# Glances ahead of the second tanh, looks in two pairs, and earlier x loads in a gated graph network kernel

## The chip, the core and the metric

The kernel runs on one core of a Trainium2 chip. The metric is device time in microseconds (us). Before the change three runs took 1787.79, 1788.79 and 1789.32 us, so the median is 1788.79.

## What is computed

For 16 graphs of 1024 nodes and 128 channels, two layers are applied, each behind a layer norm and a relu, and each added to its input. The first is a gated graph network of four steps; the second is four graph convolutions, each with a batch norm over all graphs. Cut to what matters:

```python
# layer 0: gated, per graph
h = relu(layernorm(x))
for i in range(4):
    m = adj.T @ (h @ weight[i])
    r = sigmoid(m @ w_ir + h @ w_hr + b_r)
    z = sigmoid(m @ w_iz + h @ w_hz + b_z)
    n = tanh(m @ w_in + b_in + r * (h @ w_hn + b_hn))
    h = (1 - z) * n + z * h
x = x + h * mask
# layer 1: convolutions
h = relu(layernorm(x))
for i in range(4):
    h = relu(adj @ (h @ W[i]) + b[i])
    h = gamma[i] * (h - mean(h)) / sqrt(var(h) + eps) + beta[i]
x = x + h
```

The adjacency holds only zeros and ones in this data. The kernel has a fast path that needs values whose low 16 bits are zero, and a general path that is taken at the end if any value had other low bits. So every adjacency row is inspected once, beside the work.

## The kernel before

**Two streams.** In the gated layer two graphs are in flight: stream `sa` takes the even graphs, `sb` the odd ones. A half-step (`half_step(one, two)`, called in turn with the roles swapped) does the gates of one step of stream `two` on ScalarE (ACT) and VectorE (DVE), and the aggregation of one step of stream `one` on TensorE (PE). On PE a half-step is 12 gate products of 128x512 (`products`, L993, two matmuls each) for the two halves of the nodes, hf = 0 and 1, and then 32 aggregation matmuls (`aggregate_rows`, L524). A graph takes four steps, so eight half-steps make one period, in which both streams finish a graph and start the next. The streams are one half-step apart.

**The gates of one half.** `reset_gate` is the r sigmoid on ACT (L1011), then two DVE operations, r * (g_hn + b) (L1012) and the sum with g_xn (L1013). `candidate` is the tanh on ACT (L1016), `update_gate` the z sigmoid on ACT (L1020). `less` (L1029), and the product and sum in `mixed` (L1033, L1034), are on DVE. Then `half_away` transposes the new half on DVE (L720) and sends it to HBM, from where it is read back in another layout for the next step (`cross_h`, `n_h`, `pair_out`, `pair_in`, `h_in`). The four PSUM banks g_r, g_z, g_hn and g_xn are used by both halves in turn: PE may write g_hn of the second half only when L1012 of the first has read it, and g_z only when the z sigmoid has. `high` and `low` (L926 or L942, tile ghw) split the aggregation's input of the other stream in two parts, on ACT and DVE. At the end of a half-step ACT copies the aggregation out of PSUM (tile m, L955); the next half-step's products need m.

**Rows of the next graph.** In the half-step with a stream's last gates (`self.i == 3`), `fetch` loads the first four of the next graph's eight adjacency rows (512 KB each, SyncE queue, SP, L572) into four staging buffers. `first_four` rounds them on GpSimd (POOL, L577). `last_four`, called after the second z sigmoid, inspects the four on ACT (`glance`: an activation with an accumulated sum, L586), loads rows 4 to 7 into the same four buffers, each behind the glance and the rounding that free it, and rounds them. Rows 4 to 7 of `sa` are inspected in the next half-step on DVE (`look`: a maximum over the row, L610), those of `sb` in the next half-step on ACT. Both streams share the four buffers, so `fetch` of `sb` waits for the looks at the rows of `sa`.

**The order.** In this part the order on each engine is the order of the program. Work that belongs beside another half-step is put on an agenda: `at(n, place, go)` files it, `due(place)` runs it when half-step n comes to that place. Places in order are ins, start, beside0 (after `reset_gate(0)`), mid (after `half_away(0)`, behind a small POOL copy, pace), beside1 (after `reset_gate(1)`), outs, gap and end (after `half_away(1)`). The looks at `sa` rows are at start, ahead of all gates on DVE; the glances at `sb` rows 4 to 7 are at gap, ahead of the copy of m on ACT.

**The input x of a coming graph.** `plan` files its load (`next_load`, POOL queue, L539) at mid of half-step n + 5, its statistics on DVE (L664) at start of n + 6. The tile it uses is freed by the graph that ends: its `blocks` (ACT, L680) read it last, at beside0 and beside1 of n + 4. POOL also casts rows to bf16 (tile half, L615) for the transposes of the adjacency that SP issues, and stores them (adjT_d), xmid and ymid.

Of the kernel before, what the change touches and what calls it, by code (L numbers as in the profile page):

```python
# [341 lines left out]
def exact_path(  # L342
# [24 lines left out]
    NB = N // P  # L367
# [165 lines left out]
    with ExitStack() as st:  # L533
# [36 lines left out]
        def stage_rows(b, stage, js):  # L570
            for j in js:
                nc.sync.dma_start(stage[j % 4], adj[b][j * P : (j + 1) * P, :])  # L572
# [7 lines left out]
        def glance(b, stage, js):  # L580

            junk = work.tile([P, N], BF16, tag="junk", name=f"junk{b}_{js[0]}", bufs=1)
            for j in js:
                lows = stage[j % 4].bitcast(U16).rearrange("p (n t) -> p n t", t=2)[:, :, 0]
                k = b * NB + j
                nc.scalar.activation(junk, lows, AF.Copy, accum_out=low[:, k : k + 1])  # L586
# [19 lines left out]
        def look(b, row, j, part=0):  # L606

            lows = row.bitcast(U16).rearrange("p (n t) -> p n t", t=2)[:, :, 0]
            k = (b + part * B) * NB + j
            nc.vector.tensor_reduce(low[:, k : k + 1], lows, axis=AX.X, op=ALU.max)  # L610
# [67 lines left out]
        def norm_blocks(xt, y, nt, ks):  # L678
            for k in ks:
                nc.scalar.activation(  # L680
                    y[:, k * P : (k + 1) * P], xt[:, k, :], AF.Relu, bias=nt[3][:, k, :], scale=nt[2][:, k, :]
                )
# [43 lines left out]
        def tail_sums(b, xt, hT, parts=None):  # L726

            for hf in range(NH):
                if parts:
                    pt = by_nodes(parts[hf])  # L730
                else:
                    pt = tmp(f"pt_x{b}_{hf}")
                    for q in range(BH):
                        k = hf * BH + q
                        nc.tensor.transpose(pt[:, q * P : (q + 1) * P], hT[:, k * P : (k + 1) * P], ident)
                    pt = four_ways(pt)
                for q in range(BH):
                    k = hf * BH + q
                    xk = xt[:, k, :].rearrange("p (a c) -> p a c", a=4)
                    mask = maskT[:, b * NB + k : b * NB + k + 1]  # L740
                    nc.vector.scalar_tensor_tensor(xk, pt[:, q, :, :], mask, xk, ALU.mult, ALU.add)
            return norm_stats(xt, f"mid{b}")
# [5 lines left out]
        def y_mid(b):  # L748
            return work.tile([P, N], F32, tag="h", name=f"y_mid{b}", bufs=7)
# [20 lines left out]
        class Stream:  # L770
# [54 lines left out]
            def plan(self, n, tail=None):  # L825

                if tail:
                    b, xt, hT, parts = tail
                    end = {}

                    def sums():
                        end["norm"] = tail_sums(b, xt, hT, parts)

                    def blocks(hf):
                        if hf == 0:
                            end["y"] = y_mid(b)
                        norm_blocks(xt, end["y"], end["norm"], range(hf * BH, (hf + 1) * BH))

                    at(n + 2, "gap", sums)
                    at(n + 3, "mid", lambda: store_xmid(b, xt))  # L840
                    at(n + 3, "gap", lambda: norm_factors(end["norm"]))
                    at(n + 4, "beside0", lambda: blocks(0))
                    at(n + 4, "beside1", lambda: blocks(1))
                    at(n + 5, "mid", lambda: store_ymid(b, end["y"]))
                if self.b + 2 < B:
                    at(n + 5, "mid", self.next_load)
                    at(n + 6, "start", self.next_sums)
                    at(n + 6, "gap", self.next_factors)
                    at(n + 7, "beside0", lambda: self.next_blocks(0))
                    at(n + 7, "beside1", lambda: self.next_blocks(1))  # L850
                    at(n + 7, "end", self.ins_away)

            def fetch(self):

                if self.i == 3 and self.b + 2 < B and not written[0]:
                    if self is sa:
                        t = turned_tile(f"stage{self.b + 2}").bitcast(F32)
                        room[0] = [t[:, 2 * q : 2 * q + 2, :].rearrange("p a n -> p (a n)") for q in range(4)]
                    self.stage = room[0]
                    stage_rows(self.b + 2, self.stage, range(4))  # L860

            def first_four(self):
                if self.stage:
# [2 lines left out]
            def last_four(self):  # L866
                if self.stage:
                    b, stage, self.stage = self.b + 2, self.stage, None
                    glance(b, stage, range(4))
                    stage_rows(b, stage, range(4, NB))  # L870
                    self.rows += round_rows(b, stage, range(4, NB))

                    def looks():
                        for j in range(4, NB):
                            look(b, stage[j % 4], j)

                    if self is sa:
                        at(clock[0] + 1, "start", looks)
                    else:
                        at(clock[0] + 1, "gap", lambda: glance(b, stage, range(4, NB)))  # L880

            def take(self):
                self.xt, self.y = self.next_x, self.next_y
# [173 lines left out]
        clock = [3]  # L1057

        def at(n, place, go):
            agenda.setdefault((n, place), []).append(go)  # L1060

        def due(place):
            for go in agenda.pop((clock[0], place), ()):
                go()

        def first_step(one, two, gated, halfway):

            feed.next_step()
            if one is sa:
                feed.jobs = transposes([(s.b, s.rows) for s in (sa, sb)])  # L1070
            one.split_step()
            feed.some(2)
            two.gate_step(0)
            two.half_away(0)
            if feed.full or (clock[0], "mid") in agenda:
                mids(two)
            feed.some(1)
            two.gate_step(1)
            two.half_away(1)
            gated()  # L1080
            one.agg_step(0)
            halfway()
            feed.some(NB if one is sa else 1)
            one.agg_step(1)
            two.finish()
            clock[0] += 1
# [8 lines left out]
        def half_step(one, two, gated=None, halfway=None):  # L1095

            feed.next_step()
            counts = (2, 1, 1)
            if one is sb and one.i == 0:
                feed.jobs = transposes([(s.b, s.rows) for s in (sa, sb)])  # L1100
                counts = (0, 0, 0)
            elif two is sb and two.i == 0:
                counts = (2, 2, 1)
            elif two is sa and two.i == 1 and two.across:
                counts = (3, 1, 1)
            due("ins")
            due("start")
            if one.i > 0:
                one.halves_back()
            else:  # L1110
                one.hw = hw_tiles(one.b, f"ghw{one.b}_0")
            two.fetch()
            feed.some(counts[0])
            two.products(0)
            two.reset_gate(0)
            due("beside0")
            two.candidate(0)
            two.less(0)
            one.high(0)
            two.update_gate(0)  # L1120
            one.low(0)
            two.mixed(0)
            two.half_away(0)
            two.first_four()
            if feed.full or (clock[0], "mid") in agenda:
                mids(two)
            one.high(1)
            feed.some(counts[1])
            two.products(1)
            two.reset_gate(1)  # L1130
            due("beside1")
            one.low(1)
            two.candidate(1)
            two.less(1)
            two.update_gate(1)
            two.last_four()
            two.mixed(1)
            two.half_away(1)
            due("outs")
            due("gap")  # L1140
            due("end")
            if gated:
                gated()
            one.agg_step(0)
            if halfway:
                halfway()
            feed.some(counts[2])
            one.agg_step(1)
            two.finish()
            clock[0] += 1  # L1150

        sa, sb = Stream(0), Stream(1)
        every = {getattr(mybir.EngineType, e) for e in ("PE", "DVE", "Activation", "Pool", "SP")}
        prep = st.enter_context(tc.tile_pool(name="prep", bufs=1))
        with tc.manual_schedule(engines=every):
# [20 lines left out]
            stage = keep.tile([P, NB, N], BF16, tag="adjT", name="stage", bufs=1).bitcast(F32)  # L1176
            quarters = [[stage[:, 2 * j : 2 * j + 2, :].rearrange("p a n -> p (a n)")] for j in range(4)]
            late = [[work.tile([P, N], F32, tag="h", name=f"first{j}", bufs=7)] for j in range(4, NB)]
# [404 lines left out]
```

## Time and profile before

| | |
|---|---|
| median of three runs | 1788.79 us |
| the profiled execution, its own time | 1789.26 us |
| its span, first to last instruction | 1787.5 us |
| mean granted TensorE clock | 0.999 |
| a glance on ACT (84 of them) | 1.057 us and 0.187 us to read the sum |
| a look on DVE at a staged row | 1.220 us |
| staged row load, issue to landing | 3.5 / 5.7 / 7.9 us (least, median, most) |
| waits of the statistics for x | 15.8 us, 14 times |

Times are from the page, from the answers on single tiles, and from the timeline, whose first two columns are the start and the duration in us, followed by engine, line, operation, written and read tiles, shape and count; in brackets stands the idle time of the engine before it and what ended it. Lines of POOLq, SPq and ACTq are queue entries, DMA issues among them. Positions in the run are in us from the span's start. The gated part runs from the start to about 1175 us, the convolutions from there.

### The profile page before, as it was taken

The page shows a single profiled execution, that of the slowest core. Times are in us where ns is not written, and L with a number is a line of the kernel's source. Part 1 is how long each engine was busy: PE and PEld are TensorE (multiplying, and loading weights), DVE is VectorE, ACT ScalarE, POOL GpSimd, SP SyncE. Part 2 cuts the span into 40 slices and gives each one's busy share as a digit, 9 for nine tenths or more (in the row PEclk, how much of TensorE's full clock was granted, in tenths as well). Part 3 has the DMA queues.
Part 4 walks back from the last instruction along what each step waited for, and adds up shares of the span by engine and source line. Part 5 has one row for each costly group of instructions (what it writes and reads, how often), then busy time and mean ns, then how long its engine had stood idle before and what let it go on. Part 6 is the DMA issues. An engine that isn't in the chain of part 4 may idle for free. (4 is left out here: it accounts for less than half of the span.)

```text
span 1787.5 us, 22335 instructions
## 1 busy us (share of the span) xinstructions
PE 1759.3 (98%) x6734; PEld 1191.7 (67%) x6734; DVE 1305.9 (73%) x2310; ACT 1107.6 (62%) x1713; POOL 379.3 (21%) x417
## 2 busy tenths in 40 slices
PE   9999999999999999999999999999999999999997
PEld 6565655565656565556555556577778888888886
DVE  7677877887887787887797787676666666666665
ACT  5356556556566556665655655476777767768765
POOL 4314323332331331422432333010100000000011
PEclk9999999999999999999999999999999999999999
DMA  7467657777676676776756768788766575767667
GB/s 259 135 175 262 189 163 272 179 208 241 204 200 213 223 212 197 245 202 202 260 169 186 265 174 227 256 287 311 271 228 241 207 253 201 245 224 245 238 217 268
DMA packets 363617, 400.16 MB, mean 224 GB/s; under 512 B 158188, under 2 KB 239888, under 8 KB 363488
## 3 DMA queue, kind: packets, MB, share of 16 engines
q1 hardware_dynamic: 342736, 323.59, 57.6%
q0 software_dynamic: 20224, 74.80, 11.3%
q8 instruction: 55, 0.90, 0.2%
q14 instruction: 74, 0.61, 0.1%
q10 hardware_dynamic: 528, 0.26, 0.0%
HBM read 267.47 MB, written 97.52 MB: 204 GB/s over the span
## 5 line engine op out<-in xcount | busy, mean ns | idle before, releaser
L524 PE MATMUL pm<-row,ghw 128*128 128x512 f32 x2048 | 503.6, 402 | 0.7 <-DVE ghw L926 0.6
L524 PEld LDWEIGHTS pm<-row,ghw 128*128 128x128 f32 x2048 | 383.8, 188 | 106.6 <-issue 29.2
L1016 ACT ACTIVATE r<-r,vecs 128x512 f32<-128x512 f32 x128 | 92.6, 723 | 255.0 <-DVE r L1013 253.1
L524 PE MATMUL pc_m<-wide,chw 128*128 128x512 f32 x1024 | 245.3, 395 | 0.0
L615 POOL CAST half<-row 128x1024 bf16<-128x1024 f32 x128 | 147.4, 1161 | 361.1 <-DMA adjT<-half 347.9
L524 PEld LDWEIGHTS pc_m<-wide,chw 128*128 128x128 f32 x1024 | 190.4, 188 | 41.9 <-issue 3.8
L524 PE MATMUL pc_g_r<-wide,chw 128*128 128x512 f32 x464 | 186.9, 403 | 0.3 <-ACT chw L501 0.3
L524 PE MATMUL pc_g_z<-wide,chw 128*128 128x512 f32 x464 | 181.0, 390 | 0.0
L577 POOL CAST row<-stage 128x1024 fp32r<-128x1024 f32 x112 | 128.6, 1156 | 243.7 <-DMA stage<-in_adj_dram 232.2
L1012 DVE SCALAR_TENSOR_TENSOR r<-g_hn,vecs,r 128x512 f32<-128x512 f32 x128 | 93.3, 729 | 117.9 <-ACT r L1011 66.9
L955 ACT COPY m<-pm 128x512 f32<-128x512 f32 x128 | 68.4, 585 | 163.5 <-PE pm L524 163.5
L1313 DVE CAST wide<-block 128x1024 fp32r<-128x1024 bf16 x160 | 109.9, 692 | 75.5 <-PE pc_m L524 48.3
L1313 DVE CAST wide<-packed 128x1024 fp32r<-128x1024 bf16 x160 | 110.1, 691 | 71.9 <-PE pc_g_z L524 53.5
L1311 ACT CAST wide<-packed 128x1024 fp32r<-128x1024 bf16 x96 | 100.6, 1048 | 58.5 <-PE pc_m L524 29.7
L993 PE MATMUL g_r<-m,w_mT 128*128 128x512 f32 x256 | 132.0, 597 | 3.4 <-ACT m L955 2.9
L1311 ACT CAST wide<-block 128x1024 fp32r<-128x1024 bf16 x96 | 100.7, 1049 | 53.9 <-PE pc_g_z L524 27.7
L993 PE MATMUL g_z<-m,w_mT 128*128 128x512 f32 x256 | 130.7, 592 | 0.0
L993 PE MATMUL g_xn<-m,w_mT 128*128 128x512 f32 x256 | 130.7, 592 | 0.0
L1361 DVE BATCH_NORM_STATS2 stats<-feat 128x6 f32<-128x512 f32 x128 | 84.1, 686 | 47.0 <-ACT feat L1360 45.9
L1029 DVE TENSOR_TENSOR h<-h,r 128x512 f32<-128x512 f32 x96 | 83.8, 872 | 41.9 <-ACT r L1016 41.8
L1033 DVE TENSOR_TENSOR h<-h,z 128x512 f32<-128x512 f32 x128 | 107.8, 842 | 6.8 <-ACT z L1020 0.2
L1011 ACT ACTIVATE r<-g_r,brz 128x512 f32<-128x512 f32 x128 | 87.9, 686 | 39.1 <-PE g_r L993 38.8
(186 smaller groups left out, 2830.5 us busy)
## 6 DMA issues: line engine op xcount, KB each, us to landing
block<-adjT_d SPq DMA_DIRECT2D x256, 256.0 KB, 4.7
packed<-adjT_d SPq DMA_DIRECT2D x256, 256.0 KB, 5.5
stage<-in_adj_dram SPq DMA_DIRECT2D x120, 512.0 KB, 5.7
adjT_d<-adjT POOLq DMA_DIRECT2D x16, 2048.0 KB, 7.7
cross_h<-t_h SPq DMA_DIRECT2D x92, 256.0 KB, 2.2
n_h<-cross_h SPq DMA_DIRECT2D x368, 64.0 KB, 2.0
xmid_d<-x POOLq DMA_DIRECT2D x16, 512.0 KB, 6.9
y<-ymid_d POOLq DMA_DIRECT2D x16, 512.0 KB, 5.4
```

Of the source, the lines that this page charges most:

```text
L524: nc.tensor.matmul(pm[hf], hw[s][:, j * P : (j + 1) * P], rows[j][:, hf * HALF : (hf + 1) * HALF], start=(j == 0 and s == 0), stop=(j == N ...
L577: nc.gpsimd.tensor_copy(t, stage[j % 4])
L615: nc.gpsimd.tensor_copy(t, row.bitcast(F32))
L993: nc.tensor.matmul(po, wT[:, i, g * C : (g + 1) * C], rhs, start=start, stop=stop)
L1011: nc.scalar.activation(r, pr, AF.Sigmoid, bias=brz[:, 3 * i : 3 * i + 1])
L1012: nc.vector.scalar_tensor_tensor(r, phn, b_hn(i), r, ALU.add, ALU.mult)
L1016: nc.scalar.activation(self.r, self.r, AF.Tanh, bias=b_in(self.i))
L1029: nc.vector.tensor_sub(ho, hin, self.r)
L1033: nc.vector.tensor_mul(ho, ho, self.z)
L1311: nc.scalar.copy(r, t)
L1313: nc.vector.tensor_copy(r, t)
L1361: nc.vector.bn_stats(stats[:, b * NH + hf, :], dst)
```

## The change

It changes when rows are inspected and loaded, and when x is loaded:

- `fetch` loads rows 0 and 1 only; rows 2 and 3 are loaded in a new `fetch_more`, after `reset_gate(0)`.
- `first_glances` inspects rows 0 and 1 on ACT after `reset_gate(1)`, in front of the second half's tanh. `last_four` inspects rows 2 and 3 where it inspected all four.
- The looks at rows 4 to 7 of `sa` become two pairs: 4 and 5 at start, 6 and 7 at a new place looks, behind `reset_gate(0)` and ahead of `fetch_more`.
- The glances at rows 4 to 7 of `sb` become two pairs: 4 and 5 at beside1, 6 and 7 at gap.
- `next_load` moves from mid of half-step n + 5 to a new place late of n + 4, right behind beside1. The two half-steps at the start in which it was the only thing at mid lose their pace copy.

In the built program PE and SP have the same instructions in the same order as before.

```diff
-                    at(n + 5, "mid", self.next_load)
+                    at(n + 4, "late", self.next_load)
...
                     self.stage = room[0]
-                    stage_rows(self.b + 2, self.stage, range(4))
+                    stage_rows(self.b + 2, self.stage, range(2))
+
+            def fetch_more(self):
+                if self.stage:
+                    stage_rows(self.b + 2, self.stage, range(2, 4))
...
                     b, stage, self.stage = self.b + 2, self.stage, None
-                    glance(b, stage, range(4))
+                    glance(b, stage, range(2, 4))
                     stage_rows(b, stage, range(4, NB))
                     self.rows += round_rows(b, stage, range(4, NB))
 
-                    def looks():
-                        for j in range(4, NB):
-                            look(b, stage[j % 4], j)
-
                     if self is sa:
-                        at(clock[0] + 1, "start", looks)
+                        for place, js in (("start", (4, 5)), ("looks", (6, 7))):
+                            at(clock[0] + 1, place, lambda js=js: [look(b, stage[j % 4], j) for j in js])
                     else:
-                        at(clock[0] + 1, "gap", lambda: glance(b, stage, range(4, NB)))
+                        for place, js in (("beside1", (4, 5)), ("gap", (6, 7))):
+                            at(clock[0] + 1, place, lambda js=js: glance(b, stage, js))
+
+            def first_glances(self):
+                if self.stage:
+                    glance(self.b + 2, self.stage, range(2))
...
             two.gate_step(1)
             two.half_away(1)
+            due("late")
             gated()
...
             due("beside0")
+            due("looks")
+            two.fetch_more()
             two.candidate(0)
...
             due("beside1")
+            two.first_glances()
+            due("late")
             one.low(1)
             two.candidate(1)
```

## The prediction, made before the changed kernel ran

> **What bounds the kernel now.** I read the page first, then who waited for whom with the PE filter, then the timeline of single half-steps, then the `low`, `stage` and `x` tiles.
>
> ```profile
> PE 1759.3 (98%) x6734; PEld 1191.7 (67%) x6734; DVE 1305.9 (73%) x2310; ACT 1107.6 (62%) x1713; POOL 379.3 (21%) x417
> PE g_z L993 <- ACT z L1020: 5.0, 8, 0.7
> PE g_hn L993 <- DVE r L1012: 4.6, 6, 1.2
> PE g_r L993 <- ACT m L955: 2.9, 4, 1.0
> ```
>
> PE is the bound, and its idle time is nearly all in three waits of the gated part (us in total, times, longest). These idle figures are too small, because the end of a matmul is modelled. I therefore count from start to start in the PE timeline. A gate matmul starts 0.429 us after the one before it (24 per half-step), an aggregation matmul 0.227 us after (32 per half-step): 24 x 0.429 + 32 x 0.227 = 17.56 us. Indeed 38 of the half-steps from 98 us on last 17.57 us, measured from the first g_r<-h to the next half-step's. That is the floor, and no edit here touches PE. What is above it repeats every eight half-steps, seven times, in three neighbours, which I call B, C and D (A is the half-step before B):
>
> - B (starts 151.0, 293.4, 437.0, 580.1, 725.1, 866.8, 1010.5): 19.07, 19.95, 19.65, 19.64, 18.33, 19.02, 19.95. Above the floor: 1.50 + 2.38 + 2.08 + 2.07 + 0.76 + 1.45 + 2.38 = 12.62 us.
> - C (170.0, 313.3, ...): 0.32 + 0.33 + 0.38 + 0.36 + 0.35 + 0.35 + 0.38 = 2.47 us.
> - D (187.9, 331.2, 474.6, 617.7, 761.3, 903.7, 1048.4): 0 + 0.32 + 0.12 + 1.08 + 0 + 1.30 + 1.03 = 3.85 us.
>
> Together 18.94 us. Two single ones stand apart: 0.89 at 636.3 and 1.51 at 1137.3.
>
> The timeline of one B, with the loads that lead to it:
>
> ```profile
> 290.04 3.87 SPq L572 DMA_DIRECT2D stage<-in_adj_dram  x4
> 293.62 1.22 DVE L610 TENSOR_REDUCE low<-stage 128x1 f32<-128x1024 uint16 x1 [1.08 <-DMA stage<-in_adj_dram]
> 295.33 1.22 DVE L610 TENSOR_REDUCE low<-stage 128x1 f32<-128x1024 uint16 x1 [0.49 <-DMA stage<-in_adj_dram]
> 298.24 2.59 DVE L610 TENSOR_REDUCE low<-stage 128x1 f32<-128x1024 uint16 x2 [1.69 <-DMA stage<-in_adj_dram]
> 300.74 0.74 DVE L1012 SCALAR_TENSOR_TENSOR r<-g_hn,vecs,r 128x512 f32<-128x512 f32 x1
> 301.54 1.13 PE L993 MATMUL g_hn<-h,w_hhT 128*128 128x512 f32 x2 [1.15 <-DVE r L1012]
> 304.18 1.12 PE L993 MATMUL g_z<-h,w_hhT 128*128 128x512 f32 x2 [0.66 <-ACT z L1020]
> ```
>
> Four looks, each waiting for its row, keep DVE until 300.74. Only then does L1012 read the g_hn bank, which PE wants back at about 300.2 for the second half; tanh and z follow late, so g_z waits too. The looks wait because the four row loads start at 290.04 only, one per glance. The start of a D:
>
> ```profile
> 899.34 0.72 ACT L1016 ACTIVATE r<-r,vecs 128x512 f32<-128x512 f32 x1 [5.44 <-DVE r L1013]
> 900.54 1.04 ACT L586 ACTIVATE junk<-stage 128x1024 bf16<-128x1024 uint16 x1
> 904.07 1.06 ACT L586 ACTIVATE junk<-stage 128x1024 bf16<-128x1024 uint16 x1
> 905.13 1.05 ACT L955 COPY m<-pm 128x512 f32<-128x512 f32 x2
> 905.74 1.13 PE L993 MATMUL g_r<-m,w_mT 128*128 128x512 f32 x2 [1.00 <-ACT m L955]
> ```
>
> ACT idles 5.44 us in front of tanh, then does four glances after z, and the copy of m, due at 903.7, comes 1.4 us late. The start of a C is the same in small (0.35).
>
> **What the Trainium skill says.** "Perfetto Trace Analysis", Tensor Engine Instruction (MATMUL, LD_WEIGHTS): the end of a matmul is an estimate, and ACT and DVE are strict FIFO. The trace agrees: PE counts as busy 18.09 of 19.90 us in a B that is 2.38 above the floor, and L1012 stands behind looks that it doesn't need. "SBUF — State Buffer", SBUF: two separate sides: DVE and GpSimd take a shared port pair exclusively, and the loser blocks. The trace agrees in kind: ghw at 648.36 took 3.05 us in place of 0.69 beside two POOL casts (648.83 to 650.85), which is the 0.89 at 636.3. "DMA: Bandwidth & Descriptors", Issuing engines are not separate DMA queues: POOL's x loads interleave with SP's row loads on the same engines; no run here shows their price apart.
>
> **The change part by part.** It adds no arithmetic: 84 glances and 28 staged looks are only moved. PE's and SP's order of instructions stays, POOL loses two pace copies of 0.19 us.
>
> *A's glances.* On ACT, y_in ends at 285.13 and tanh starts at 287.63 after an idle 2.50. A glance takes 1.18 from start to start (288.83, 290.00, 291.19), so two take 2.36 and fit; their rows have landed, since POOL casts the first from 282.36 and the second before 284.9. Tanh is not moved. Cost 0; were the rows late, tanh would shift by all lateness over 0.14, but it may end as late as 290.4, since z (0.6) and now only two glances (2.36) come before m is due at 293.4.
>
> *A's row loads.* Rows 4 and 5 now go when the first two glances end: 286.6 and 287.5 in place of 290.04 and 291.23. Rows 6 and 7 wait for the glances after z, 290.0 and 291.2 in place of 292.41 and 293.59. With the lags of before (3.6, 4.1, 5.8 and 6.0 us from issue to look) they land at 290.2, 291.6, 295.8 and 297.2. The next on SP (pair_out, pair_in, h_in) moves up 2.4 us with them.
>
> *B's looks.* DVE's transposes end at 292.5. Looks 4 and 5: to 295.0. The r sigmoid ends at 295.96, so L1012 runs to 296.7 (PE needs it at 300.2: 3.5 spare) and L1013 to 297.4. Tanh and one cast later z ends at 299.3; PE asks for g_z's bank at 301.9 (2.6 spare). Looks 6 and 7, now behind L1013: to 299.9. They make the subtraction L1029 wait 1.8, and L942, which it holds back, ends at 301.1; the aggregation needs that at 303.3. So B falls to its floor: 12.62. If row 4 and 5 were no earlier, L1012 would still be at 296.6, so this gain doesn't hang on the loads.
>
> *B's glances, the one new wait.* The two before the second tanh wait for the other stream's rows 0 and 1. Their loads stood at 299.67 behind row 7's landing and SP's h_in; now row 7 lands at 297.2 and looks 4 and 5 are done. So issue at about 297.3 and 298.0, landing with 6.3 and 5.8 us (299.67 to the cast at 306.00; 301.47 to 307.23) at 303.6 and 303.8. Glances end at 304.8 and 306.0. Queued behind them are tanh, z, two glances and the copy of m. Tanh's input is ready at 304.6 (L1012 and L1013 after t_out at 303.2), up to 306.2 if two DVE operations share with POOL casts at 1.5 us in place of 0.7. Tanh at 306.2, z until 307.5, glances until 309.9; m is due at 310.9. C's 2.47 goes, with 1.0 spare.
>
> *C's glances.* Two fill ACT's idle time before tanh (4.5 to 5.4 us), their rows landed long before. Two are left in the gap: z ends at 900.6, they at 903.0, m due 903.7. D's 3.85 goes, with 0.7 spare in the worst D.
>
> *x earlier.* POOL issues it (0.90) 15 to 17 us sooner, at about 217.2 in place of 232.92. It waits for blocks that ended at 214.93 and is behind POOL's xmid store, so it waits for nothing. Two casts behind it start 0.9 later; POOL idles 9.89 after them. The statistics lose their wait for x (15.8 us of DVE, 14 times), but those half-steps stand at 17.57, so I count 0. Without that cover the casts could push a port collision onto a ghw: 0.9 each time, or take away the one at 636.3: from -0.9 to +6.
>
> Sum: 12.62 + 2.47 + 3.85 = 18.94 less. From the profiled execution (span 1787.5, and 1.8 outside it, 1789.26) that is 1770.3; from the median 1788.79, half a microsecond lower, 1769.9. I take 1770.
>
> **The rivals.**
> - The row loads don't come earlier, because the 16 engines are the limit (DMA share 0.84 in that B). B's gain stays, D's too, but B's glances wait for rows that land at 307.2: tanh at 308.4, glances done at 312.0, m 1.1 late in each C in place of 0.35. 18.94 - 2.47 - 7 x 0.75 = 11.2 less: 1777.6. Against it: SP stood in waits for glances, not for engines.
> - No change: what B gives back is lost at the next exchange through HBM, whose cross_h and n_h transfers come no sooner. Then 1788.8, at best -3. Against: C and D wait for ACT alone.
> - Slower: B's glances hold ACT in front of tanh. They start to cost when row 1 lands after 306.1 (tanh latest 307.3), and eat all 18.94 / 7 = 2.7 per period when it lands after 308.8. Landing at 310 in every period, tanh 3.9 late, would give 7 x 3.9 = 27.3 more against 18.9 less: 1797. For it: row lags were up to 7.9 us. Against: even unadvanced it landed before 307.3.
>
> **Numbers.** Full gain (1767 to 1773.5) 0.62; partial (to 1785) 0.24; no change 0.07; slower 0.07. What a measurement can tell here is 0.2%, 3.6 us. Faster 0.86, same 0.07, slower 0.07. The low end, 1767, takes the full sum, the 0.89 and some of 1137.3; the high end, 1779, the partial case and a collision or two, leaving about 2 in 10 outside.
>
> **What would show it.** Right: B, C and D at 17.57; L1012 of a B at start + 2.7 to 3.4; row loads in two pairs some 3 us apart; no PE wait on ACT m at 313 or 903. Wrong: tanh in a B released by a glance later than start + 14; PE waiting for ACT m at the start of C; ghw of 3 us in the half-steps with x loads.

## The result and the profile after

| | before | changed |
|---|---|---|
| median, runs | 1788.82 us, 5 | 1772.93 us, 5 |
| lowest and highest | 1787.79, 1790.83 | 1772.15, 1774.21 |
| span of the profiled execution | 1787.5 us | 1772.3 us |

The ratio is 0.991, with an interval of 0.9896 to 0.9925: faster by 0.9%, or 15.9 us. The profiled execution of the changed kernel took 1774.21 us, the slowest of the five.

The page and the waits of PE of the changed kernel, in the same columns as before:

```profile
PE 1754.2 (99%) x6734; PEld 1194.8 (67%) x6734; DVE 1288.6 (73%) x2310; ACT 1108.6 (63%) x1713; POOL 373.0 (21%) x415
PE g_z L999 <- ACT z L1026: 3.6, 4, 1.8
PE g_r L999 <- ACT m L961: 0.3, 1, 0.3
```

The wait of g_hn for DVE is gone, the one of g_r for m is down to 0.3 us, but g_z still waits for z four times, with a longest wait of 1.8 us that the kernel before didn't have. Counted from start to start in the PE timeline, all seven B, all seven C and all seven D last 17.57 us. New time stands elsewhere: in three half-steps at 222.8 (19.70 us), 365.5 (17.93) and 506.4 (18.53), which are the second half-step after D. I call this place E; before the change the first E started at 223.1, and every E lasted 17.57. The fourth half-step, at 80.0, takes 19.77 in place of 18.74; like an E it follows an adjT_d store.

The timeline of the B that was shown of before, with the A in front of it, in the changed kernel (A starts at 277.6, B at 295.2):

```profile
286.87 1.04 ACT L586 ACTIVATE junk<-stage 128x1024 bf16<-128x1024 uint16 x1
288.08 4.92 SPq L572 DMA_DIRECT2D stage<-in_adj_dram  x4
293.91 2.30 DVE L610 TENSOR_REDUCE low<-stage 128x1 f32<-128x1024 uint16 x2
298.04 0.75 DVE L1018 SCALAR_TENSOR_TENSOR r<-g_hn,vecs,r 128x512 f32<-128x512 f32 x1 [1.82 <-PE g_hn L999]
299.50 2.34 DVE L610 TENSOR_REDUCE low<-stage 128x1 f32<-128x1024 uint16 x2
302.06 1.02 PE L999 MATMUL g_hn<-h,w_hhT 128*128 128x512 f32 x2
304.94 1.06 ACT L586 ACTIVATE junk<-stage 128x1024 bf16<-128x1024 uint16 x1 [1.99 <-DMA stage<-in_adj_dram]
307.22 0.71 ACT L1022 ACTIVATE r<-r,vecs 128x512 f32<-128x512 f32 x1
```

The first glance runs in front of tanh, and the first row load follows it at A + 10.5 (before: A + 14.3). The first pair of looks no longer waits for anything. L1018, which was L1012, now waits for PE and not the other way round, and the second pair of looks runs after it. The g_hn matmul follows without a gap. The glance at 304.94 waited 1.99 us for its row, and tanh still comes in time.

The start of the D shown of before:

```profile
884.09 1.05 ACT L586 ACTIVATE junk<-stage 128x1024 bf16<-128x1024 uint16 x1
888.14 0.72 ACT L1022 ACTIVATE r<-r,vecs 128x512 f32<-128x512 f32 x1 [1.74 <-DVE r L1019]
890.51 1.06 ACT L586 ACTIVATE junk<-stage 128x1024 bf16<-128x1024 uint16 x1
893.97 1.07 ACT L961 COPY m<-pm 128x512 f32<-128x512 f32 x2 [2.31 <-PE pm L524]
```

Two glances now fill most of the idle time in front of tanh (1.74 us are left of 5.44), two follow z, and ACT then waits 2.31 us for PE before it can copy m.

The worst E, from the stores in the half-step in front of it:

```profile
218.30 0.89 POOL L629 DMA_DIRECT2D adjT_d<-adjT  x1 [2.97 <-DMA adjT<-half]
219.18 0.89 POOL L752 DMA_DIRECT2D xmid_d<-x  x1
220.06 0.89 POOL L539 DMA_DIRECT2D x<-in_x_dram  x1
222.20 10.49 SPq L598 DMA_DIRECT2D n_h<-cross_h  x8
232.09 0.62 ACT L925 CAST ghw<-n_h 128x512 fp32r<-128x512 f32 x1 [3.94 <-DMA n_h<-cross_h]
232.62 0.68 ACT L1026 ACTIVATE z<-g_z,brz 128x512 f32<-128x512 f32 x1
233.35 1.12 PE L999 MATMUL g_z<-h,w_hhT 128*128 128x512 f32 x2 [1.83 <-ACT z L1026]
```

POOL issues 2 MB of adjT_d, 512 KB of xmid and now 512 KB of x in a row. Behind them SP asks for n_h, the new state in the layout that the aggregation needs. It lands late: x lands at 231.2, and the first four n_h loads at 231.4 to 231.9. The `cross_h` store that SP issued just before them, which the other four n_h loads wait for, took 9.1 us to land, against 3.1 at the same place before. The cast that waits for n_h stands in front of z on ACT, and PE waits for z. The `n_h` tile says the same of the whole run; before, then the changed kernel:

```profile
DMA to landing us min/median/max: 1.8/2.0/6.8
```

```profile
  DMA n_h<-cross_h: 29.4, 23
DMA to landing us min/median/max: 1.8/2.1/9.3
```

The median is the same, the longest landing is not, and engines now wait 29.4 us for n_h in place of 6.1.

### The profile page after: what moved, and what is told of

The parts are those of the page before. It is cut to its first block, busy times and chain, and to the rows that moved or that the text cites. A ratio compares the mean times of both kernels' runs of the same rounds, so it can differ in the third digit from the quotient of the medians.

```text
span 1772.3 us, 22314 instructions
## 1 busy us (share of the span) xinstructions
PE 1754.2 (99%) x6734; PEld 1194.8 (67%) x6734; DVE 1288.6 (73%) x2310; ACT 1108.6 (63%) x1713; POOL 373.0 (21%) x415
## 5 line engine op out<-in xcount | busy, mean ns | idle before, releaser
L615 POOL CAST half<-row 128x1024 bf16<-128x1024 f32 x128 | 141.9, 1120 | 397.8 <-DMA adjT<-half 384.6
L1018 DVE SCALAR_TENSOR_TENSOR r<-g_hn,vecs,r 128x512 f32<-128x512 f32 x128 | 93.6, 731 | 136.9 <-ACT r L1017 75.5
L1035 DVE TENSOR_TENSOR h<-h,r 128x512 f32<-128x512 f32 x96 | 83.3, 868 | 41.7 <-ACT r L1022 41.7
```

Source lines behind the costliest of these rows:

```text
L615: nc.gpsimd.tensor_copy(t, row.bitcast(F32))
L1018: nc.vector.scalar_tensor_tensor(r, phn, b_hn(i), r, ALU.add, ALU.mult)
L1035: nc.vector.tensor_sub(ho, hin, self.r)
```

## The experiments

My theory after the result: the looks and glances do all that was forecast, and what is missing comes from `sa`'s x load, whose bytes delay the n_h that follows. Rivals: the earlier row loads delay n_h; POOL's issue of the load shifts its casts and the transposes; or it was chance. The table gives, for the profiled execution of each run, the sum in us above 17.57 of all B, all C, all D and the half-steps at E's place (seven with the last period's, which has no x load), the excess of the fourth half-step over 18.74, and the median of the timed runs. The kernel before spread more widely beside these runs than beside the first (medians of 1789.9 to 1792.2), so I compare the sums first, and medians only where they were taken together.

| run | B | C | D | E | fourth | median us | ratio to before |
|---|---|---|---|---|---|---|---|
| before | 12.62 | 2.47 | 3.86 | 0.03 | 0 | 1788.82 | 1 |
| changed | 0.02 | 0.02 | 0.02 | 3.47 | 1.03 | 1772.93 | 0.991 [0.9896, 0.9925] |
| both x loads back | 0.02 | 0.02 | 0.03 | 0.83 | 0 | 1770.81 | 0.989 [0.9874, 0.9907] |
| x alone early | 13.83 | 3.58 | 2.37 | 2.42 | 1.12 | 1794.0 | 1.0018 [1.0001, 1.0035] |
| sa's x back | 0.02 | 0.02 | 0.03 | 0.03 | 0 | 1770.24 | 0.9888 [0.9871, 0.9904] |
| an eighth of x early | 0.02 | 0.02 | 0.02 | 0.68 | 0 | 1769.57 | 0.9884 [0.9868, 0.9901] |
| looks alone | 0.02 | 0.64 | 1.83 | 0.68 | 0 | 1773.56 | 0.9908 [0.9883, 0.9934] |
| glances alone | 1.10 | 0.02 | 0.02 | 0.92 | 0 | 1770.98 | 0.9886 [0.9865, 0.9907] |
| changed, again | 0.02 | 0.02 | 0.02 | 1.79 | 0.65 | 1772.61 | 0.9899 [0.9879, 0.9919] |
| sa's x twice | 0.02 | 0.02 | 0.02 | 11.16 | 1.83 | 1785.18 | 0.9965 [0.9952, 0.9978] |
| sa's x back, again | 0.02 | 0.02 | 0.02 | 1.01 | 0 | 1770.56 | 0.9885 [0.9865, 0.9905] |
| z first | 0.02 | 0.02 | 0.02 | 7.70 | 0.95 | 1778.12 | 0.9933 [0.9919, 0.9947] |
| z first, sa's x back | 0.02 | 0.02 | 0.02 | 1.05 | 0 | 1771.67 | 0.9903 [0.9889, 0.9916] |

**The x load, taken back and taken alone.** Both loads back to mid of n + 5, in the changed kernel:

```diff
-                    at(n + 4, "late", self.next_load)
+                    at(n + 5, "mid", self.next_load)
```

> The changed kernel with the x load back at mid of half-step n + 5. Theory (the new stalls before g_z, 2.13 + 0.36 + 0.96 us in the half-steps at 222.8, 365.5 and 506.4 and 0.60 at 80.0, come from sa's x load standing right behind the adjT_d and xmid stores, so that the next n_h loads land late): these stalls vanish, B, C and D stay at 17.57 us, and the time falls by 3.5 to 5 us from 1772.9, to 1768 to 1769.5. Rival (the earlier row loads and glances themselves push the n_h exchange): the stalls stay, 1772 to 1774.

Measured: no stall in any E of the first six periods, the fourth half-step is at 18.74 again, B, C and D stay. What is left at E is in the last period, where no x is loaded: there POOL issued adjT_d only 1.95 us before the half-step began, and the n_h loads landed behind it and xmid. Seven of the runs have this last stall (0.66 to 1.04 us), all with adjT_d issued 1.8 to 2.2 us ahead; in the kernel before, the changed one and the run with `sa`'s x back it went 4.7 to 5.1 us ahead, and they don't stall there. The span is 1768.7, the median 1770.81, above the expected 1768 to 1769.5. The rival falls: with the earlier rows and glances, and x back in its place, n_h stalls none of the six E that have an x load.

The reverse, only the x load and its place late, on the kernel before:

> The kernel before with the x load alone moved to late of n + 4. Theory: B, C and D keep their 18.9 us above the floor, and half-steps three after C get stalls before g_z that sum to 2 to 5 us: 1791 to 1794, slower than before by 0.1 to 0.3%. Rival (x load harmless, stalls come from the other edits): 1788 to 1789.5, no g_z stall in those half-steps.

```profile
PE g_z L993 <- ACT z L1020: 6.0, 10, 0.7
PE g_hn L993 <- DVE r L1012: 5.9, 6, 1.5
PE g_r L993 <- ACT m L955: 2.8, 5, 1.0
```

All three waits of the kernel before are there, g_z with two more. Stalls at E and in the fourth half-step sum to 3.54, but 1.27 of that is in the last period, which has no x load: there the last two n_h loads were issued just after a 256 KB load of w_hhT and landed just after it (at start + 11.3 and 11.5, w_hhT at 11.1). The 2.27 left are at the low end of what was expected. The median is 1794.0, ratio 1.0018 with an interval that just excludes 1. That the x load by itself costs is shown by the half-steps more than by the median.

**Which x load.** `sa`'s back, `sb`'s kept early:

```diff
-                    at(n + 4, "late", self.next_load)
+                    if self is sa:
+                        at(n + 5, "mid", self.next_load)
+                    else:
+                        at(n + 4, "late", self.next_load)
```

> The changed kernel with sa's x load back at mid of n + 5, sb's kept at late of n + 4. Theory (only the x load that shares a half-step with the adjT_d store hurts): no stall before g_z, 1768 to 1769.5 like the run with both back. Rival (either early x load hurts): half of the loss stays, 1770 to 1772.

E and the fourth half-step are clean. The median of 1770.24 lies in the rival's range, but the half-steps decide: no part of the stalls stays, and the run with both loads back, beside it, was no faster (1770.81). So `sb`'s early load is harmless. `sa`'s is the one that shares its half-step with the adjT_d store; that this is what tells them apart is argued from their places, and no run shows it alone.

**Bytes or queue place.** An eighth of x at late of n + 4, the rest at mid of n + 5:

```diff
-                    at(n + 4, "late", self.next_load)
+                    at(n + 4, "late", lambda: self.load_part(0, 1))
+                    at(n + 5, "mid", lambda: self.load_part(1, NB))
```

> The changed kernel with an eighth of x (64 KB) loaded at late of n + 4 and the other seven eighths at mid of n + 5: POOL issues a transfer at the same place as in the changed kernel, but with few bytes. Theory (the bytes in front of the n_h loads are the cause): the g_z stalls shrink to 0.6 us or less in all, 1768 to 1770. Rival (POOL's 0.9 us of issue shifts the casts and so the transposes and SP's order): stalls stay at 3 to 4.5 us, 1772 to 1773.5.

The stalls at E are gone but for 0.68 in the last period. POOL still issues a transfer there; with 64 KB it does no harm. The median of 1769.57 is as the theory has it. The other way, the same bytes twice:

```diff
                 self.next_x = load_x(self.b + 2, nc.gpsimd)
+                if self is sa:
+                    spare = dram.tile([N, C], F32, tag="spare", name=f"spare{self.b}")
+                    nc.gpsimd.dma_start(spare, x[self.b + 2])
```

> The changed kernel with a second transfer of the same 512 KB right behind sa's x load (DRAM to DRAM, into a spare buffer that nothing reads; it adds traffic, the output is unchanged). Theory (bytes ahead of the n_h loads): n_h lands some 2 us later in each half-step E (three after C). In the changed kernel the first ghw of the six E began at start + 9.97, 8.24, 8.84, 6.97, 7.32 and 7.06 and stalls began at about + 7.85, so all six stall, 10 to 14 us in sum, and the fourth half-step 2 us more: 1779 to 1786. Rival (the place in POOL's queue, not the bytes): 0.9 us of issue more, at most 3 us in sum: 1773 to 1776.

```profile
PE g_z L1002 <- ACT z L1029: 9.4, 8, 2.8
```

Beside it the changed kernel had 3.6 us in 4 waits. The six E last 18.39, 19.15, 19.91, 18.17, 22.25 and 17.83, 10.28 us above the floor, at the low end of the 10 to 14 expected; the excess of the fourth half-step is 1.83, up by 0.80 where 2 more were expected. The median is 1785.18. All six stall, as expected of bytes, and by more than the 3 us that a place in the queue could explain. The longest landing of an n_h load is 10.5 us.

**Chance, and the better version on the same chip.**

> The changed kernel once more, beside the two that follow on one chip. Theory: the g_z stalls again in the half-step three after C of some periods and in the fourth half-step, in sum 3 to 5 us; 2 to 4 us slower than the version with sa's x load put back. Rival (they were chance of one execution): no such stalls, the two versions equal within 1 us.

> The version with sa's x load back at mid of n + 5 and all else as changed, timed on the same chip as the changed kernel. Theory: 2 to 4 us faster than the changed kernel, E at 17.57 throughout. Rival: within 1 us of it.

Changed 1772.61, `sa`'s x back 1770.56: 2.05 us faster, at the low end of what was expected. The changed kernel again stalls in the second and third E (17.77, 18.11) and in the fourth half-step (19.39), but not in the first E, which was the largest before. At the places with an x load this is 1.39 us in sum, under the 3 to 5 expected. The rest of its 1.79 at E is the last period's stall; the version with `sa`'s x back has that too (0.99), so its E are not at 17.57 throughout, as I had expected.

The size is not mere chance: it goes with how late POOL issues adjT_d. In these two executions of the changed kernel, the store was issued 4.47, 5.33, 5.87, 5.92 and 6.06 us before the E that stalled by 2.13, 0.96, 0.54, 0.36 and 0.20 us; in the seven E that didn't stall it was issued 6.35 us or more before. Time alone doesn't do it: with `sa`'s x back, the first E lasted 17.57 with the store 4.96 us ahead. With x alone early two small stalls, of 0.22 and 0.17 us, came with the store 7.31 and 6.56 us ahead, so the order isn't strict. The store waits for the transposes of the adjacency; why they end later in some periods is not shown.

The half-step in front of the first E, in the version with `sa`'s x back:

```profile
216.62 0.89 POOL L629 DMA_DIRECT2D adjT_d<-adjT  x1 [2.68 <-DMA adjT<-half]
217.50 0.89 POOL L752 DMA_DIRECT2D xmid_d<-x  x1
221.45 6.74 SPq L598 DMA_DIRECT2D n_h<-cross_h  x8
227.37 0.62 ACT L928 CAST ghw<-n_h 128x512 fp32r<-128x512 f32 x1 [0.42 <-DMA n_h<-cross_h]
227.89 0.68 ACT L1029 ACTIVATE z<-g_z,brz 128x512 f32<-128x512 f32 x1
230.16 1.02 PE L1002 MATMUL g_z<-h,w_hhT 128*128 128x512 f32 x2
```

Without the third transfer SP issues its eight n_h loads within 6.74 us in place of 10.49, the cast waits 0.42 in place of 3.94, and z ends before PE asks for its bank. This version beats both kernels.

**The looks and the glances, each alone** on the kernel before. The looks in pairs with `fetch_more`, cut (`fetch` loads rows 0 and 1 only, as in the changed kernel):

```diff
-                        at(clock[0] + 1, "start", looks)
+                        for place, js in (("start", (4, 5)), ("looks", (6, 7))):
+                            at(clock[0] + 1, place, lambda js=js: [look(b, stage[j % 4], j) for j in js])
...
             due("beside0")
+            due("looks")
+            two.fetch_more()
```

> The kernel before with the looks in two pairs alone, and rows 2 and 3 fetched behind the second pair; all glances and the x load as before. Prediction (B's gain doesn't hang on the loads): B falls to within 0.3 us of 17.57, its 12.6 us come back; C keeps about 0.3 each and D its 3.85: 1775 to 1777.5. Rival (the looks still wait for rows that come late): B keeps a third or more of its excess, 1780 to 1785.

The glances, with `first_glances` and, not shown here, the pairs at beside1 and gap:

```diff
-                    glance(b, stage, range(4))
+                    glance(b, stage, range(2, 4))
...
+            two.first_glances()
             one.low(1)
```

> The kernel before with the glances alone split (two in front of the second tanh, those for sb in two pairs), which also brings row loads 4 and 5 forward by 3.4 us; looks all four at start, x load as before. Theory: C and D fall to 17.57; the last look ends at about start + 5.0 in place of + 7.4, L1012 is in time for PE, but tanh and z come late for g_z by 0.3 to 0.8 us in each B: 1771.5 to 1775. Rival (with four looks in front B keeps its stall): 1780 to 1784.

The wait of PE for m with the looks alone, and then its wait for z with the glances alone:

```profile
PE g_r L994 <- ACT m L956: 1.7, 5, 0.4
```

```profile
PE g_z L998 <- ACT z L1025: 1.7, 3, 0.6
```

Either takes nearly all of B away: with the looks alone 0.02 is left, with the glances alone 1.10. C and D need the glances; with the looks alone they keep 2.47 of 6.33. That is less than I expected (C some 0.3 each and D 3.85, so 1775 to 1777.5, measured 1773.56). Gates that are on time in B may leave the later glances more room, but no run shows that apart. The glances alone came out at 1770.98, just below the 1771.5 to 1775 expected: in the B of before that was shown, the last look now ends at B + 5.4 in place of 7.5. So the edits overlap: 16.5 us by the looks and 17.8 by the glances, each by themselves, and 18.9 together. By its ratio the run with the glances alone, 0.9886, does as well as the best versions here, so the looks in pairs add little once the glances are split.

**A remedy that failed.** On ACT, z in front of the cast that waits for n_h, in the changed kernel, and the same with `sa`'s x back:

```diff
-            one.high(0)
             two.update_gate(0)
+            one.high(0)
             one.low(0)
```

> The changed kernel, sa's x load still early, with one edit on ACT: the z sigmoid of the first half stands in front of the cast that waits for n_h, not behind it. Theory (late n_h hurts PE only because that cast holds z): n_h lands as late as in the changed kernel, but PE no longer waits for z in the E half-steps; where n_h comes latest (ghw at start + 9.3) the aggregation may wait up to 1 us instead. 3 to 4.5 us come back: 1768 to 1770. Rival (late n_h is needed by the aggregation itself at once): the stalls move to pm, 1772 to 1774.

> Both remedies together: z in front of the cast, and sa's x load back at mid of n + 5. Theory: nothing left to gain in E, so at most the single g_z wait of 1 us near 1070 goes as well: 1768.5 to 1770.5, within 1.5 us of either remedy alone. Rival (the cast behind z delays the aggregation in ordinary half-steps): slower than 1771, with waits of pm for ghw.

The waits of PE in the first of the two:

```profile
PE pm L524 <- DVE ghw L932: 5.1, 6, 1.5
PE g_z L999 <- ACT z L1026: 0.6, 1, 0.6
```

The first took 1778.12 us, slower than the changed kernel, with stalls in all six E. One half of the theory holds: z was held by the cast in front of it, for the g_z waits shrink from 3.6 to 0.6. The other half fell. The rival was right on the place, for the stalls move to pm, but not on the size, 1772 to 1774. At about start + 14.2 the aggregation waits for the second ghw. n_h itself had landed by then: in the E at 365.2 its last load lands at start + 10.75. The second cast follows on ACT, the r sigmoid stands behind that cast, and the second ghw stands on DVE behind the two operations that need r; it starts at start + 13.61. In five of the six E it then took 1.4 to 1.8 us in place of 0.7. With `sa`'s x back as well, 1771.67, pm waits three times, 1.8 us in all. That is the rival's picture again, so the order of before is the better one. The late landing has to be cured, not what stands behind it.

## Why the prediction was right, and where it was short

- **The floor and what is above it.** Right: every B, C and D fell to 17.57, the full 18.94. The single 0.89 at 636.3, which I did not count, went too, and it was the early x load that took it away, as shown below.
- **A's glances and row loads.** Right. Predicted at A + 10.8, 11.7, 14.2 and 15.4; measured in the execution of after at A + 10.46, 11.65, 13.87 and 15.05.
- **B's looks.** Right, L1012 at B + 2.6 predicted and 2.85 measured. That B's gain doesn't hang on the loads is shown by the run with the looks alone. What I did not see is that it hardly hangs on the looks either: with the glances alone all but 1.10 of it came.
- **B's glances, the new wait.** Right: rows 0 and 1 were predicted to land at B + 10.2 and 10.4, and the first glance began at B + 9.75, after a wait of 1.99. Tanh was predicted at B + 12.8, measured at 12.0.
- **C's glances.** Right, and with more room: in the worst D 0.7 us to spare were forecast; at the same place ACT now waited 2.31 us for PE.
- **x earlier.** This step failed. I priced it at 0, with a range of -0.9 to +6 from collisions of POOL's casts with ghw. I looked for what stands behind it in POOL's queue and for its cover on DVE, and found none to wait. What it delays is on another queue: SP's n_h loads, issued some 2 us after it, behind 3 MB instead of 2.5 MB from POOL. That cost 2.13 + 0.36 + 0.96 in three E and 1.03 in the fourth half-step, 4.48 in the profiled execution, and 0.20 + 0.54 in two E and 0.65 in the fourth half-step, 1.39, in the second one. The sentence of the Trainium skill that I cited ("DMA: Bandwidth & Descriptors", Issuing engines are not separate DMA queues), that transfers of all queues interleave on the same engines, was the one to price: the trace agrees, with n_h loads of SP landing after up to 9.2 us behind POOL's three transfers in the worst E.
- **What the early x gave back.** The one gain that the range allowed, -0.9, came true. Before, the second ghw of the half-step at 636.3 was held up by two POOL casts, though it had started 0.47 us before the first of them. In the changed kernel POOL issues x first, and the casts start after that ghw is done; before, then the changed kernel:

```profile
648.36 3.05 DVE L926 TENSOR_TENSOR ghw<-n_h,ghw 128x512 fp32r<-128x512 f32 x1
648.83 2.02 POOL L615 CAST half<-row 128x1024 bf16<-128x1024 f32 x2
```

```profile
641.57 0.68 DVE L932 TENSOR_TENSOR ghw<-n_h,ghw 128x512 fp32r<-128x512 f32 x1
642.02 0.89 POOL L539 DMA_DIRECT2D x<-in_x_dram  x1
642.91 2.02 POOL L615 CAST half<-row 128x1024 bf16<-128x1024 f32 x2
```

In all seven executions with `sa`'s x at mid of n + 5 this ghw took 3.05 us and the half-step lost 0.24 to 0.90; in all six with a transfer at its early place, the 64 KB included, it took 0.68 to 1.36 and nothing was lost. The casts now hold up the DVE operation behind it (L1035, 3.04 us), and PE doesn't wait for that. So POOL's time to issue helps, and the bytes hurt.

- **The sum.** 18.94 + 0.89 - 4.48 = 15.35; the span fell by 15.2. The early x thus cost 3.6 us net. That is inside the range I gave it, but by luck: the range was made of collisions, and n_h was not in it. The forecast of 1770 was 2.9 us low of the median, near the upper end of what I called the full gain (1767 to 1773.5). The versions without the early `sa` load measured 1770.24, 1770.56 and 1770.81; the one with an eighth of x early, which has neither the bytes nor the collision, 1769.57, the lowest median of all.
- **The rivals.** "The row loads don't come earlier" and "slower by late rows" are refuted by the times above. "What B gives back is lost at the next exchange through HBM" was right on the place, the n_h and cross_h transfers, and wrong on the cause and the size: it was x, not B.

## What to carry to other kernels

A transfer that is moved to an earlier place can have a cost at a small, urgent transfer that is issued next, on another queue too; look for the next dependent read through HBM before you call an early bulk load free. When a PE-bound kernel shows a floor per step, count each step from start to start and sum what is above it: that number is the most that a change off PE can give, and a step with a new excess points to the cost. Two fixes of one wait can overlap, so test each alone before crediting either.

## What was not expected of the hardware

Small reads of 64 KB, whose landing had a median of 2.0 us, took up to 9.2 us in an E when 3 MB had been issued on another queue 2 to 4 us before, and up to 10.5 us with 3.5 MB. With 2.5 MB, whose issue began 4.6 to 7.8 us before the half-step, no E stalled in any run that kept the order of ACT; with the same 2.5 MB begun only 1.8 to 2.2 us before it, in the last period, the reads took up to 8.0 us and PE lost 0.66 to 1.04. So it is both the bytes and how shortly before they are issued. The same 512 KB was free as `sb`'s load and cost up to 2.1 us as `sa`'s, one half-step earlier.
